# Attention and gated layers on one core: the weight comparison moved ahead of the first exponentials, the second key fill moved to ScalarE, the last norm split over two steps

## The chip, the cores and the metric

The kernel runs on one core of a Trainium2 chip. A core has five engines that run their own instruction streams and wait for each other through semaphores: TensorE (PE in the profile: matrix products and transposes, results in PSUM), VectorE (DVE), ScalarE (ACT: activation functions), GpSimd (POOL) and SyncE (SP, which here only starts DMA transfers). ACT starts DMAs too. The metric is the device time of one execution in microseconds; lower is better.

## The reference

32 sequences of 256 tokens, 128 features. One causal attention layer of 16 heads of 8 features with a linear decay, a residual and a layer norm; then a chain of five scaled linear layers, a residual and a second norm. All in float32.

```python
Q, K, V = (split_heads(x @ W.T + b) for W, b in ((Wq, bq), (Wk, bk), (Wv, bv)))
scores = einsum('bhid,bhjd->bhij', Q, K) / sqrt(8)
scores = where(j > i, -inf, scores) - (i - j)        # decay by distance
out = (softmax(scores) @ V).reshape(B, T, D) @ Wo.T + bo
x = layernorm(x + out)
h = silu((x @ w1.T) * s1) * ((x @ w2.T) * s2)        # 128 -> 512
h = gelu((h @ h1.T) * sh1)                           # 512 -> 512
h = gelu((h @ h2.T) * sh2)                           # 512 -> 512
x = layernorm(x + (h @ w3.T) * s3)                   # 512 -> 128
```

The matrices `w1`, `w2`, `h1`, `h2`, `w3` come out of the setup with whole-number entries.

## The kernel before

**Tiles.** Two sequences make a *pair* (512 tokens); there are 16 pairs, and the main loop is `step(n)` for n = 0 to 15. For each pair the queries and keys of all heads lie in two large tiles, `qs` and `ks` (128 partitions x 8 groups x 512 tokens), of which there are two each, used in turn by even and odd pairs. A head takes 8 rows of features, each stored as a rounded part and a remainder (`qhi`, `qlo`, `khi`, `klo`), further rows with constants that bring in the decay, and two rows for the row maxima. The constant rows are written once into each of the four tiles by `fill`; `stack` then copies a pair's features into their rows with four DMAs of 256 KB for q and four for k.

**One pair's work.**
- `project(n)`: loads the x of pair n + 1, transposes x (`pxT`, `xT`), multiplies by Wq and Wk (`pq`, `pk`) and splits the results into `hi` (ACT) and `lo` (DVE). POOL adds the bias `bo` to x.
- `row_maxima(n, i)`, i = 0 to 11: scores in one orientation into a PSUM tile, then a DVE reduction to `m` (the profile's `m<-s`). `maxima_to_rows(n)`: transposes `m` (`pm`), splits it (`mhi`, `mlo`) and copies it with DMAs into the rows of `qs`.
- `weigh(n, i)`, i = 0 to 11: scores in the other orientation with the maxima taken off, exp on ACT (`e`), causal zeroing on POOL (`e<-e`). Score tiles and the tiles of the layers share three PSUM buffers of two banks, in turn.
- `outputs(n, a)`: `e` times the values (`pa`), a copy (`oT`), a transpose (`pt`), the division (`rec`, `on`). `project_values` makes the values (`pv`, `vaug`).
- `finish(n)`: transposes `on` (`pon`, `onT`), multiplies by Wo (`po`) and adds x. `first_norm(n)`: statistics (`sta`, `mva`, `rsa`), a power on POOL, the scaled x. `turn(n)`: its transpose (`px1T`, `x1T`).
- `feed(n)`: the four 512-wide layers on `x1T`: `pw` and `sg`, `h0w`, `h`; then `podd`, `hodd` and `peven`, `heven`. With exact weights the activations are again a rounded part and a remainder, made by ACT (twice) and DVE (the remainder), and every product has both.
- `last(n)`: the `w3` product (`pw` on `heven`), a copy `yT`, a transpose `py`, the residual `y`, the last norm (`stf`, `mvf`, `rsf`, a power on POOL, `z`) and the store of `z`.

**Order.** There is no planner at work: engines keep the order in which the program issues instructions, which is written out by hand with generators. `step(n)` first runs twelve slots: in slot i it weighs tile i of pair n, takes maximum tile i of pair n + 1, and lets `project(n + 2)`, `last(n - 2)` and the outputs advance at given slots. Then it runs `feed(n - 1)`; between two pieces of it one piece of `rest()` is issued, in this order: the remaining outputs, `maxima_to_rows(n + 1)`, the values of pair n + 2, `finish(n)`, `first_norm(n)` and what is left of `last(n - 2)`, that is its norm's statistics in one slot and `z` in the next. `LEAD` and `LAG` shift the maxima: 2 tiles of pair 1 come before step 0, and in step 1 the maxima of pair 2 start 3 slots late, the last three go into `rest`.

**The opening.** Before the loop come the constants, `project(0)`, the fills, the stacks of pairs 0 and 1, and the maxima of pair 0. `ks0` is filled by ACT, `qs0` and `qs1` by DVE, `ks1` by POOL. The weight matrices are loaded (`load_layers`, SP) in the middle of the maxima of pair 0.

**The branch on the weights.** `inexact_weights` rounds the five matrices, in 11 pieces of 512 columns (ACT copies `w_near`, `h_near`), compares each with its original (DVE, `differ`) and counts the differences into `number`. Its pieces are issued between the slots of step 0. After step 0, which has no `feed`, each engine loads `number` and branches: with no difference the rounded weights are used as they are (this is the branch taken with these inputs), otherwise full float32 weights are loaded again. Steps 1 to 15 are inside the branch.

**DMA.** SP and ACT each issue in order. Eight completion semaphores are used in turn by both, so that a DMA is issued only when the one eight places before it has landed.

Of the kernel before, what the change touches and what calls it, by code (L numbers as in the profile page):

```python
# [33 lines left out]
G, C = 4, 4  # L34


LEAD, LAG = 2, 3
VHEAD = HD + 1
VSLOT = 3 * VHEAD
VCOLS = H // 2 * VSLOT + 32 + VHEAD - VSLOT  # L40
HID = 512
# [20 lines left out]
def tile_attn_ffn(  # L62
# [47 lines left out]

    qs = [const.tile([P, W, TOK], F32R, name=f"qs{i}") for i in range(2)]
    ks = [const.tile([P, W, TOK], F32R, name=f"ks{i}") for i in range(2)]
    sctx = ctx.enter_context(ExitStack())
    setup = sctx.enter_context(tc.tile_pool(name="setup", bufs=1))

# [111 lines left out]
    for i in range(2):  # L227
# [7 lines left out]


    layers = (
        ("w1", w1T, 1, HID), ("w2", w2T, 1, HID), ("h1", h1T, KC, HID), ("h2", h2T, KC, HID),
        ("w3", w3T, KC, D),
    )  # L240
    near = {
        nm: const.tile([P, k, o], F32R, name=f"{nm}_near") for nm, _, k, o in layers
# [3 lines left out]
        sc[nm] = const.tile([P, KC], F32, name=nm)  # L246
    sc["s3"] = const.tile([P, 1], F32, name="s3")

    def load_layers(pool):
        got = {}  # L250
        for nm, src, k, o in layers:
            got[nm] = pool.tile([P, k, o], F32, name=f"{nm}_sb")
            sp.dma_start(out=got[nm], in_=src.rearrange("(k p) o -> p k o", p=P))
        return got
# [412 lines left out]
    def run(gen):  # L667
        for _ in gen:
            pass


    ahead = project(0)
    next(ahead)
    constants("q", q)
    fill(qs[0], "q", vec)
    run(ahead)
    stack(0, "q", sp)
    stack(0, "k", act)
    fill(ks[1], "k", nc.gpsimd)
    ahead = project(1)  # L680
    next(ahead)
    fill(qs[1], "q", vec)
    run(ahead)
    stack(1, "q", sp)
    stack(1, "k", act)
    project_values(0)
    for a in range(G):
        act.dma_start(
            out=wo_sb[C * HD * a : C * HD * (a + 1), :],
            in_=woT[:, :, a, :].rearrange("c d o -> (c d) o"),  # L690
        )
    sctx.close()
    ep = enter(tc.tile_pool(name="ep", bufs=5))
    op = enter(tc.tile_pool(name="op", bufs=2))
    yp = enter(tc.tile_pool(name="yp", bufs=2))
    lctx = ctx.enter_context(ExitStack())
    once = lctx.enter_context(tc.tile_pool(name="once", bufs=1))
    for i in range(6):
        row_maxima(0, i)
    project_values(1)  # L700
    maxima_to_rows(0, (0,))
    loaded = load_layers(once)
    for i in range(6, 3 * G):
        row_maxima(0, i)
    maxima_to_rows(0, (1,))
    load_scales()
    for i in range(LEAD):
        row_maxima(1, i)

    def step(n, exact=None, ws=None, hp=None, gp=None):  # L710


        side = iter(())
        settling = (
            last(n - 2, exact, ws, gp) if n > 1 else first_norm(0) if n else inexact_weights()
        )
        ahead = project(n + 2) if n + 2 < NPAIR else iter(())
        for i in range(3 * G):
            weigh(n, i)
            j = i + {0: LEAD, 1: -LAG}.get(n, 0)  # L720
            if n + 1 < NPAIR and 0 <= j < 3 * G:
                row_maxima(n + 1, j)
            next(side, None)
            if n and i == 9:
                turn(n - 1, exact)
            if i in ((0, 2) if n > 1 else (0, 2, 4, 6)) if n else i < 11:
                next(settling, None)

            if i in ((3, 4, 5) if n == 1 else (1, 3, 5)):
                next(ahead, None)  # L730
            if i % 3 == 2:
                run(side)
                side = outputs(n, i // 3)
            if n == 0 and i == 3 * G - LEAD:
                maxima_to_rows(1)
        if n < 2:
            run(settling)
        run(ahead)
        if n + 2 < NPAIR:
            stack(n + 2, "q")  # L740
            stack(n + 2, "k", sp if n else act)


        def rest():
            for _ in range(3):
                next(side)
                yield
            if n == 1:
                for i in range(3 * G - LAG, 3 * G):
                    row_maxima(2, i)  # L750
                    yield
            if 0 < n < NPAIR - 1:
                maxima_to_rows(n + 1)
            run(side)
            yield
            if n + 2 < NPAIR:
                project_values(n + 2)
                yield
            last_steps = finish(n)
            next(last_steps)  # L760
            yield
            yield from last_steps
            if n:
                yield
                yield from first_norm(n)
            if n == NPAIR - 1:
                yield
                turn(n, exact)
            if n > 1:
                yield  # L770
                yield from settling

        if n:
            prepare(AF.Silu)
        due = rest()
        for _ in feed(n - 1, exact, ws, hp, gp) if n else ():
            next(due, None)
        run(due)

    def others(exact, ws, hp, gp):  # L780
        for n in range(1, NPAIR):
            step(n, exact, ws, hp, gp)

        settling = last(NPAIR - 2, exact, ws, gp)
        for i, _ in enumerate(feed(NPAIR - 1, exact, ws, hp, gp)):
            if i in (3, 4, 8, 9):
                next(settling, None)
        run(last(NPAIR - 1, exact, ws, gp))

    step(0)  # L790
    inexact = nc.values_load(
        pairs.pop("inexact"), min_val=0, max_val=P * HID * 11,
        skip_runtime_bounds_check_because="it is only compared with zero",
# [68 lines left out]
```

## Time and profile before

| | |
|---|---|
| time, median of 3 runs | 848.8 us (848.36 to 851.17) |
| the profiled execution's own time | 849.53 us |
| its span, first to last instruction | 847.2 us |
| mean granted TensorE clock | 0.978 |
| busy: PE, DVE, ACT, POOL | 789.4, 642.9, 525.1, 276.1 us |
| DMA moved | 47.49 MB |
| ACT table loads | 47 of 1283 ns |
| maxima reductions, 128 | 155.5 us, 1218 ns each |
| exponentials, 128 | 130.5 us, 1020 ns each |
| one step in the middle, start to start | 48.74 us |
| first maxima product; first product of steps 0, 1, 2 | 30.02; 49.74, 85.79, 136.80 us |

A line of the timeline gives the start in us from the span's start, the duration, the engine, the source line (L58 is a helper that issues most instructions), the operation, output <- inputs by the program's names, the shapes, a count, and in brackets the engine's idle time before it with what ended it. PEld is the loading of weights into TensorE. A window line gives the stretch and its length, then the busy time of PE, PEld, DVE, ACT and POOL with their instruction counts, the granted TensorE clock, the busy share of the DMA engines and GB/s. In the table of slices each digit is one fortieth of the span, in tenths.

### The profile page before, as it was taken

To read this page: it belongs to the slowest core of one execution; us is meant where nothing else is said; L and a number is where in the kernel's file an instruction comes from. 1 tells how busy PE (TensorE), PEld (TensorE's weight loads), DVE (VectorE), ACT (ScalarE), POOL (GpSimd) and SP (SyncE) were. 2 spreads that over 40 slices of the span, in tenths; PEclk is the share of its full clock that TensorE was granted. 3 is DMA by queue.
4 is the path that set the end of the run, shared out by engine and by line. 5 is a ranking of instruction groups with operands and counts; after the bars stand their busy time and mean duration, and the time that the engine had idled before them with its cause. 6 is when DMAs were issued, how large, how long until landed. Compare 5 with 4: busy or idle time off the path is not lost.

```text
span 847.2 us, 17426 instructions
## 1 busy us (share of the span) xinstructions
PE 789.4 (93%) x7046; PEld 553.1 (65%) x7046; DVE 642.9 (76%) x1245; ACT 525.1 (62%) x718; POOL 276.1 (33%) x341
## 2 busy tenths in 40 slices
PE   2897899999999999999999999999999999999985
PEld 0555576676767677676767667676766767666663
DVE  8877777877787777778878777878878777773674
ACT  3036565766666666666667676667667666668662
POOL 9023422414142432414243341424234141424210
PEclk9859999999999999999999999999999999999998
DMA  2843140411314040220404031040414013000001
GB/s 65 197 146 80 38 102 15 93 36 29 76 26 103 27 101 28 49 56 26 103 26 104 26 73 44 15 103 27 104 26 94 23 26 79 14 4 13 1 13 30
DMA packets 39882, 47.49 MB, mean 56 GB/s; under 512 B 3952, under 2 KB 21616, under 8 KB 39792
## 3 DMA queue, kind: packets, MB, share of 16 engines
q1 hardware_dynamic: 37136, 42.82, 21.3%
q10 hardware_dynamic: 2656, 3.48, 1.7%
q8 instruction: 57, 0.93, 0.5%
q14 instruction: 33, 0.27, 0.1%
HBM read 7.48 MB, written 4.19 MB: 14 GB/s over the span
## 4 chain that ended last, share of the span: by engine, by line
PE 73%; DVE 10%; ACT 4%; POOL 3%; issue 1%; DMA 1%; SPq 0%; ACTq 0%; POOLq 0%; DVEq 0%
PE podd L58 13%; PE pa L58 11%; PE s L58 10%; PE peven L58 8%; PE pw L58 8%; DVE heven L58 4%; POOL rsf L273 2%; PE s_2d L58 2%; PE s_3d L58 2%; PE s_1d L58 2%; PE s_0d L58 2%; PE po L58 2%; DVE z L58 2%; PE pt L58 2%; PE pk L58 2%; PE pq L58 2%
## 5 line engine op out<-in xcount | busy, mean ns | idle before, releaser
L58 DVE TENSOR_REDUCE m<-s 128x4 f32<-128x1024 f32 x128 | 155.5, 1218 | 9.1 <-PE s L58 7.8
L58 ACT ACTIVATE e<-s 128x1024 f32<-128x1024 f32 x128 | 130.5, 1020 | 45.0 <-PE s L58 25.4
L462 POOL TENSOR_SCALAR_AFFINE_SELECT e<-e 128x512 f32<-128x512 f32 x128 | 84.7, 662 | 184.3 <-ACT e L58 156.2
L58 PE MATMUL podd<-h,h_near 128*128 128x512 f32 x512 | 131.4, 403 | 0.9 <-DVE m L58 0.5
L58 PE MATMUL peven<-hodd,h_near 128*128 128x512 f32 x512 | 122.6, 395 | 0.0
L58 PEld LDWEIGHTS peven<-hodd,h_near 128*128 128x128 f32 x512 | 95.8, 187 | 23.2
L58 PEld LDWEIGHTS podd<-h,h_near 128*128 128x128 f32 x512 | 91.8, 188 | 23.0 <-DVE h L58 3.0
L58 ACT ACTIVATE hodd<-podd,sh 128x512 fp32r<-128x512 f32 x64 | 44.0, 688 | 62.8 <-PE podd L58 62.6
L58 PE MATMUL pw<-x1T,w_near 128*128 128x512 f32 x256 | 75.6, 418 | 2.2 <-DVE h0w L58 2.2
L273 POOL TENSOR_TENSOR rsa<-rsa,half 128x4 f32<-128x4 f32 x16 | 16.3, 1018 | 175.9 <-DVE rsa L58 175.9
L58 PE MATMUL pa<-e,vaug 128*32 128x256 f32 x1024 | 71.4, 393 | 0.0
L58 DVE SCALAR_TENSOR_TENSOR h0w<-pw,s,sg 128x512 f32<-128x512 f32 x64 | 47.9, 748 | 29.4 <-ACT sg L58 29.4
L58 PEld LDWEIGHTS s<-qs,ks 64*128 64x128 f32 x512 | 38.9, 188 | 47.3 <-issue 33.6
L58 DVE TENSOR_TENSOR heven<-evenw,heven 128x512 fp32r<-128x512 f32 x64 | 44.0, 688 | 29.5 <-ACT evenw L58 29.0
L58 PE MATMUL s<-qs,ks 64*128 64x256 f32 x512 | 65.3, 334 | 1.1 <-DMA qs<-qhi 0.6
L58 ACT ACT_TABLE_LOAD x47 | 60.3, 1283 | 3.4 <-issue 2.6
L58 ACT ACTIVATE sg<-pw,s 128x512 f32<-128x512 f32 x64 | 43.6, 683 | 29.0 <-PE pw L58 27.9
L58 PE MATMUL s<-ks,qs 62*128 62x256 f32 x512 | 55.1, 294 | 4.0 <-ACT e_0d L58 1.7
L58 ACT ACTIVATE heven<-peven,sh 128x512 fp32r<-128x512 f32 x48 | 33.3, 694 | 39.7 <-PE peven L58 39.7
L58 PEld LDWEIGHTS pw<-x1T,w_near 128*128 128x128 f32 x256 | 43.4, 188 | 19.5 <-ACT nothing L58 5.8
L580 POOL TENSOR_TENSOR h<-h0w,h 128x512 fp32r<-128x512 f32 x31 | 39.9, 1288 | 43.5 <-DVE h L58 41.2
L273 POOL TENSOR_TENSOR rsf<-rsf,half 128x4 f32<-128x4 f32 x16 | 21.0, 1314 | 97.1 <-DVE rsf L58 97.1
(148 smaller groups left out, 1462.4 us busy)
## 6 DMA issues: line engine op xcount, KB each, us to landing
qs<-qhi SPq DMA_DIRECT2D x32, 256.0 KB
qs<-qlo SPq DMA_DIRECT2D x32, 256.0 KB
ks<-khi SPq DMA_DIRECT2D x26, 256.0 KB
ks<-klo SPq DMA_DIRECT2D x26, 256.0 KB
x<-in_x_dram SPq DMA_DIRECT2D x16, 256.0 KB
out_dram<-z SPq DMA_DIRECT2D x16, 256.0 KB
ks<-khi ACTq DMA_DIRECT2D x6, 256.0 KB
ks<-klo ACTq DMA_DIRECT2D x6, 256.0 KB
```

The source lines that it names most:

```text
L58: return lambda *args, **kw: self.tc.keep_in_program_order(call(*args, **kw))
L273: nc.gpsimd.tensor_tensor(rs, rs, half, ALU.pow)
L462: nc.gpsimd.affine_select(out=on_diagonal, in_=on_diagonal, pattern=[[0, on_diagonal.shape[1]], [1, P]], base=0, channel_multiplier=-1, co ...
L580: (nc.gpsimd if o < (1 if final else 2) else vec).tensor_tensor(h[:, 1, o, :], whole, h[:, 0, o, :].bitcast(F32), ALU.subtract)
```

## The change

- **Fills.** `ks1` is filled by ACT instead of POOL, after three pieces of the comparison. 
- **Weights.** `w1`, `w2`, `w3` are loaded by SP right behind the x of pair 1, `h1` and `h2` behind the first q stack. `wo` and the scales go to SP behind the second q stack. The order of the layers in the comparison becomes w1, w2, w3, h1, h2.
- **Comparison and branch.** All 11 pieces are issued in the opening: three before the first maxima, six after maxima tiles 6 to 11 of pair 0, two after the first two maxima tiles of pair 1. The count, the load of `number` and the branch follow, and step 0 is now inside the branch.
- **Step 0 to step 1.** Step 0 ends after its twelve slots; its last outputs, the values of pair 2, `finish(0)` and `first_norm(0)` are issued one piece a slot in step 1 (`attended`). `stack(2, "k")` moves from ACT to SP. `LAG` is 5 instead of 3, the five maxima tiles left go into three pieces of `rest`, and `project(3)` moves from slots 3, 4, 5 of step 1 to slots 6, 7, 8.
- **Last norm.** In `rest` the statistics of `last(n - 2)` and the power are issued in the same slot as the end of `first_norm(n)`; `z` and its store wait in `late` until slot 3 of the next step (after the loop for the last one).

```diff
-LEAD, LAG = 2, 3
+LEAD, LAG = 2, 5
...
     ahead = project(0)
     next(ahead)
+    loaded = load_layers(once, layers[:3])
     constants("q", q)
     fill(qs[0], "q", vec)
     run(ahead)
     stack(0, "q", sp)
     stack(0, "k", act)
-    fill(ks[1], "k", nc.gpsimd)
+    loaded.update(load_layers(once, layers[3:]))
+    comparison = inexact_weights()
     ahead = project(1)
     next(ahead)
     fill(qs[1], "q", vec)
+    for _ in range(3):
+        next(comparison)
+    fill(ks[1], "k", act)
+    for i in range(2):
+        row_maxima(0, i)
+    next(ahead)
+    row_maxima(0, 2)
     run(ahead)
     stack(1, "q", sp)
     stack(1, "k", act)
+    row_maxima(0, 3)
     project_values(0)
+    for i in range(4, 6):
+        row_maxima(0, i)
...
+    load_scales()
+    project_values(1)
     sctx.close()
...
     maxima_to_rows(0, (0,))
-    loaded = load_layers(once)
     for i in range(6, 3 * G):
         row_maxima(0, i)
+        next(comparison)
+    prepare(AF.Exp)
     maxima_to_rows(0, (1,))
-    load_scales()
     for i in range(LEAD):
         row_maxima(1, i)
+        next(comparison)
+    run(comparison)
+    late, left = [], []
+    def attended(n, side):
+        yield from side
+        project_values(n + 2)
+        yield
+        last_steps = finish(n)
+        next(last_steps)
+        yield
+        yield from last_steps
+        yield from first_norm(n)
...
+            if i == 3 and late:
+                run(late.pop())
...
-            if i in ((3, 4, 5) if n == 1 else (1, 3, 5)):
+            if i in ((6, 7, 8) if n == 1 else (1, 3, 5)):
                 next(ahead, None)
...
-            stack(n + 2, "k", sp if n else act)
+            stack(n + 2, "k")
+        if n == 0:
+            left.append(side)
+            return
...
-            if n:
-                yield
-                yield from first_norm(n)
+            yield
+            yield from first_norm(n)
...
             if n > 1:
-                yield
-                yield from settling
+                next(settling)
+                late.append(settling)
...
     def others(exact, ws, hp, gp):
-        for n in range(1, NPAIR):
+        for n in range(NPAIR):
             step(n, exact, ws, hp, gp)
+        run(late.pop())
...
-    step(0)
     inexact = nc.values_load(
```

More of the change, by code (lines that the diff above doesn't have):

```diff
@@ L112, in tile_attn_ffn @@
     ks = [const.tile([P, W, TOK], F32R, name=f"ks{i}") for i in range(2)]
+    ep = enter(tc.tile_pool(name="ep", bufs=5))
+    op = enter(tc.tile_pool(name="op", bufs=2))
+    yp = enter(tc.tile_pool(name="yp", bufs=2))
+    lctx = ctx.enter_context(ExitStack())
+    once = lctx.enter_context(tc.tile_pool(name="once", bufs=1))
     sctx = ctx.enter_context(ExitStack())
@@ L237, in tile_attn_ffn @@
     layers = (
-        ("w1", w1T, 1, HID), ("w2", w2T, 1, HID), ("h1", h1T, KC, HID), ("h2", h2T, KC, HID),
-        ("w3", w3T, KC, D),
+        ("w1", w1T, 1, HID), ("w2", w2T, 1, HID), ("w3", w3T, KC, D), ("h1", h1T, KC, HID),
+        ("h2", h2T, KC, HID),
     )
@@ L247, in tile_attn_ffn, with load_layers @@
     sc["s3"] = const.tile([P, 1], F32, name="s3")
-    def load_layers(pool):
+    def load_layers(pool, some=layers):
         got = {}
-        for nm, src, k, o in layers:
+        for nm, src, k, o in some:
             got[nm] = pool.tile([P, k, o], F32, name=f"{nm}_sb")
@@ L685, in tile_attn_ffn @@
     stack(1, "k", act)
+    row_maxima(0, 3)
     project_values(0)
+    for i in range(4, 6):
+        row_maxima(0, i)
     for a in range(G):
-        act.dma_start(
+        sp.dma_start(
             out=wo_sb[C * HD * a : C * HD * (a + 1), :],
@@ L691, in tile_attn_ffn, with step @@
         )
+    load_scales()
+    project_values(1)
     sctx.close()
[L693 to L700, printed above, removed]
     maxima_to_rows(0, (0,))
-    loaded = load_layers(once)
     for i in range(6, 3 * G):
         row_maxima(0, i)
+        next(comparison)
+    prepare(AF.Exp)
     maxima_to_rows(0, (1,))
-    load_scales()
     for i in range(LEAD):
         row_maxima(1, i)
-    def step(n, exact=None, ws=None, hp=None, gp=None):
+        next(comparison)
[10 more added lines that the diff above has]
+        yield from first_norm(n)
+    def step(n, exact, ws, hp, gp):
         side = iter(())
         settling = (
-            last(n - 2, exact, ws, gp) if n > 1 else first_norm(0) if n else inexact_weights()
+            last(n - 2, exact, ws, gp) if n > 1 else attended(0, left.pop()) if n else iter(())
         )
@@ L725, in step @@
                 turn(n - 1, exact)
-            if i in ((0, 2) if n > 1 else (0, 2, 4, 6)) if n else i < 11:
+            if n < 2 or i in (0, 2):
                 next(settling, None)
-            if i in ((3, 4, 5) if n == 1 else (1, 3, 5)):
+            if i in ((6, 7, 8) if n == 1 else (1, 3, 5)):
                 next(ahead, None)
@@ L750, in rest @@
                     row_maxima(2, i)
-                    yield
-            if 0 < n < NPAIR - 1:
+                    if i % 2:
+                        yield
+            if n < NPAIR - 1:
                 maxima_to_rows(n + 1)
@@ L762, in rest @@
             yield from last_steps
-            if n:
-                yield
-                yield from first_norm(n)
+            yield
+            yield from first_norm(n)
             if n == NPAIR - 1:
@@ L769, in rest @@
             if n > 1:
-                yield
-                yield from settling
-        if n:
-            prepare(AF.Silu)
+                next(settling)
+                late.append(settling)
+        prepare(AF.Silu)
         due = rest()
-        for _ in feed(n - 1, exact, ws, hp, gp) if n else ():
+        for _ in feed(n - 1, exact, ws, hp, gp):
             next(due, None)
```

## The prediction

> **What bounds the kernel now.** I read the table of 40 slices, then windows, the timeline at one handover between steps, and the opening.
>
> ```profile
> PE   2897899999999999999999999999999999999985
> PEclk9859999999999999999999999999999999999998
> ```
> From slice 5 on TensorE (PE) is full: there it is the bound, and only its own stalls can be won. A window over one step:
> ```profile
> 427.88:476.62 48.74, 47.90 (x442) 33.81 (x442) 38.16 (x76) 32.31 (x44) 16.25 (x21) 1.00 0.24 56
> ```
> 48.74 us a step; VectorE (DVE) holds 38.16, ScalarE (ACT) 32.31. The timeline shows where PE stops:
> ```profile
> 427.60 1.38 POOL L273 TENSOR_TENSOR rsf<-rsf,half 128x4 f32<-128x4 f32 x1 [5.27 <-DVE rsf L58]
> 427.88 0.51 PE L58 MATMUL s<-qs,ks 64*128 64x256 f32 x4
> 429.01 1.12 DVE L58 TENSOR_SCALAR z<-y,mvf,rsf 128x128 f32<-128x128 f32 x4 [0.91 <-POOL rsf L273]
> 430.05 0.68 DVE L58 TENSOR_TENSOR heven<-evenw,heven 128x512 fp32r<-128x512 f32 x1
> 430.79 0.84 PE L58 MATMUL pw<-heven,w_near 128*128 128x512 f32 x2 [0.61 <-DVE heven L58]
> 431.85 0.49 PE L58 MATMUL pw<-heven,w_near 128*128 128x512 f32 x1 [0.22 <-DVE heven L58]
> 432.27 0.50 PE L58 MATMUL s<-qs,ks 64*128 64x256 f32 x4
> ```
> DVE waits for POOL's power and writes the last norm's z while two `heven` remainders queue behind it; PE's `w3` product (pw) waits for those. The step from pair 1 to 2 has no such norm in front:
> ```profile
> 136.80 0.50 PE L58 MATMUL s<-qs,ks 64*128 64x256 f32 x4
> 137.65 2.13 PE L58 MATMUL pw<-heven,w_near 128*128 128x512 f32 x8
> 139.71 0.50 PE L58 MATMUL s<-qs,ks 64*128 64x256 f32 x4
> ```
> 2.91 us from the first s to the second, against 4.39.
>
> The opening is bound by a DVE held up beside POOL, and the stacks' transfers:
> ```profile
> 5.58 10.62 POOL L192 TENSOR_SCALAR ks<-kconst,col_k_base 128x4096 fp32r<-128x4096 f32 x1
> 5.83 10.65 DVE L58 TENSOR_SCALAR qconst<-number_of,col_q_lo,col_q_value 128x512 f32<-128x512 f32 x1
> 30.02 0.50 PE L58 MATMUL s<-ks,qs 62*128 62x256 f32 x4 [1.32 <-DMA qs<-qlo]
> 77.59 0.14 DVE L58 CAST number<-total 1x1 int32<-1x1 f32 x1
> 85.79 0.74 PE L58 MATMUL s<-qs,ks 64*128 64x256 f32 x8 [0.58 <-DMA qs<-qhi]
> ```
> The same DVE operation on kconst took 0.58 at 2.13. Step 0 runs 49.74 to 85.79.
>
> **The change, part by part.** Times are in the profiled execution, 849.53 us (span 847.2 and 2.3 around it), 0.7 above the median, 848.8.
>
> *Second k fill to ACT.* Without POOL's 10.62, qconst's three operations (0.6 + 0.8 + 0.8) start at 5.83 and the q fill (2.43) ends near 10.5, not 20.66. The eight stack transfers (2.1 MB) are then issued 10.6 to 13.2; at 0.24 MB/us (the 22 to 30 us rows give 220 to 253 GB/s) they land at 20.9, and with as much delay as the first ones showed, 21.5. First maxima matmul 21.5 instead of 30.02: -8.5. ACT's fill (3.71 as its sister at 5.67) and three weight copies (0.61 each) end by 19, under the transfers; uncovered they cost 5.5.
>
> *Weights.* w1, w2, w3 (0.79 MB) go out on SP behind x; h1, h2 (2.1 MB) and x of pair 2 behind the first q stack. Within the queue they follow it: 0. Bound: served ahead of it, 2.36 MB at 286 GB/s (the 44 to 46 row, weights moving) costs 8.2. `wo` and the scales move from ACT to SP, behind the second q stack; the maxima rows queue behind them, but are read only at 52, and `wo` in step 1: 0, or the 5.14 that ACT's four `wo` issues took.
>
> *Comparison and branch ahead of step 0.* Between the first maxima and the branch DVE now has 14 maxima (two in 2.34: 16.4), 8 comparisons (69.28 to 71.03 is one with a maximum, 1.79 typical, so 0.62: 5.0), qlo and klo 1.5, v additions 2 x 0.89, mlo 2 x 0.68, the count 0.3: 26.4. Waits (0.7 for the first tile, qlo and klo behind products of 1.0 to 2.05, two mlo behind 1.0 to 1.6) are 1.8 to 5; I take 3.6, as PE is mostly slow here. The number stands at 51.5. Load and branch now stand in front of all: `x` ending at 86.01 and its statistics starting at 86.08 bound them below at 0.1, po's first matmul (84.05) to s (85.79) above at 1.7; I take 1.2, nearer PE's row. Step 0 starts at 52.7, +3.0 on 49.74.
>
> *Step 0 without comparisons.* PE's work to the end of pm, by the durations of the chain: 11 score tiles (8 at 0.43, 3 diagonal ones at 0.61) 5.3, 10 maxima tiles (6 at 0.42, 4 at 0.66) 5.2, the projection (0.59, 1.06, 1.06) 2.7, pa three times 1.00 + 0.57, 4.7, pt 0.6, pm 0.4: 18.9 at full clock. DVE has 15.2 of work beside it (10 maxima, xT, qlo, klo, one rec and on) and ACT 14.8 (11 exps, qhi, khi, oT, mhi), so both fit under PE; before it took 25.8 (49.74 to 75.52), half of that at clock 0.50:
> ```profile
> 32.00:34.00 2.00, 2.00 (x20) 1.21 (x20) 2.00 (x2) 0.00 (x0) 0.00 (x0) 0.50 1.07 228
> 58.00:62.00 4.00, 4.00 (x20) 1.23 (x22) 1.87 (x5) 0.56 (x2) 0.62 (x1) 0.50 0.00 0
> ```
> The clock was 0.50 for 6.4 us (from 31.9), 20.4 (from 42) and 3 (from 89.9). PE is sparse before the branch, so step 0 starts slow; I take 8.4 us, half of it lost: 4.2 (bounds 1.5 and 10.2). pm ends at 75.8.
> The Trainium skill (TensorE: Matmul & The Clock Gate, What's actually happening) says that one sustained busy window of about 3.4 us restores the full clock. The stretch at 89.9 agrees, the two longer ones, full by their rows, do not; by the rule the sum would be 2.5 lower, 827.5.
>
> *Hand-over 0 to 1.* Nothing of pair 0 stands before step 1's first s now, so it meets mhi, mlo and their transfers: 1.9 to mlo's issue (75.52 to 77.64 without the comparison between), and a landing of 0.6 to 3.3 (x: issue 0.79, read 4.10); I take 2: s at 79.7, not 85.79, though PE stands idle for some 3 us before it. The k stack on SP frees ACT of the 3.04 it waited at 77 to 80.
>
> *Step 1.* It takes over pa's end (1.57), pt, pv, pon, po from step 0 and the branch: 4.6 of PE work. Up to `pw` PE holds 12 score tiles 5.9, seven maxima tiles 3.4, pa 6.3, two pt 1.2, pv, pon, po 2.4, the projection 2.7, px1T 0.6: 22.5; the maxima of pair 2, five tiles later, still meet their stacks: issued from pm + 3.3, 9.0 to move, 2 to land is 90.1 (the 80 to 86 rows move 0.23 MB/us); PE, 8.2 into the step, is there at 87.9: 2.2 of waiting, and 0.6 of small waits like the 0.2 to 0.8 ones of step 1 now. pw at 105.0 (108.82 before). Its feed layers took 28.0; two more maxima tiles there (1.1) and podd's wait for their buffers (1.0) make 30.1: step 2 starts at 135.1 instead of 136.80. All before step 2: **-1.7**.
>
> *Last norm.* Its statistics now follow the first norm's x in DVE's gap (423.55 to 425.56), z goes behind the fourth maximum of the next step, where the line of qlo at 439.30 shows DVE idle for 1.22: z's 1.12 fits, price 0, at most 1.12. SP issues its store after the next x. heven runs as in the pair 1 to 2 step, whose second diagonal tile comes 4.47 after the first s (136.80, 141.27) against 5.83 (427.88, 433.71): 1.36 less. Next late is exp behind ACT's table load. Pairs 2 to 13 hand over so: 12 x 1.36 = **-16.3**. The hand-over 14 to 15 ends on ACT: 0. In the last step z (1.11 at 811.34) leaves its place before three heven operations but comes again before h0w; with sg, freed 0.4 earlier, h0w starts near 813.2 instead of 814.03: **-0.8**.
>
> Sum -18.8: 849.53 - 18.8 - 0.7 = **830.0**.
>
> **Rivals.**
> 1. *Weights in front of the stacks.* The transfer rows of 22 to 38 us are full, so sharing is real; queue order speaks against it. +8.2: 838.2.
> 2. *The clock comes back in 3 us*, as at 89.9, here and in the comparisons (products 1.06, not 2.05): -2.7 and -2.7: 824.6. Against it: two of the three slow stretches lasted longer. The rule of the Trainium skill (TensorE: Matmul & The Clock Gate, What's actually happening) would have it so.
> 3. *The stall only moves*: z's 1.12 pushes maxima whose buffers PE waits for, and the 16.3 come back: 846.3. Against it: the 1.22 gap.
> 4. *Slower: the clock stays halved* through step 0 and on. It decides from 46 us of slow dense work (8.4 + 2 x 18.8); the longest stretch seen is 20.4. Lasting to step 1's pw (41.4 of work, all lost again, less the 4.2) it gives 867.
> 5. *No change in effect*: none; the instruction order does move z, fill and branch.
>
> **Numbers.** Forecast 0.50, rivals 0.20, 0.20, 0.05, 0.05. A measurement tells about 0.3%; 846.3 is within it. Faster 0.90, same 0.05, slower 0.05. Range 820 (rival 2, with the short waits and early landing) to 841 (rival 1, with late branch and landing).
>
> **What would show it.** s after the first hand-over s: 2.9 us, step period 47.4; z without idle POOL wait near qlo; qconst at 0.6; first maxima near 21.5; the number near 51.5; step 1's s near 80; step 2 near 135. Wrong if PE waits appear on DVE m after z, or the granted clock is 0.50 beyond 70 us.

## The result, and the profile after

The changed kernel takes 839.25 us (median of 4 runs, 838.77 to 841.65); the kernel before took 849.98 beside it (4 runs, 848.36 to 854.79). The ratio is 0.987, with a 95% interval of 0.9824 to 0.9916: faster by 1.3%. 830.0 was forecast, with a range of 820 to 841. The profiled execution took 838.77 us, with a span of 836.9, so 10.3 us of span came off where 18.8 were forecast.

The trace gives the two halves of that apart. In the steady part everything came as forecast. The page's table of 40 slices for the changed kernel:

```profile
PE   2868899999999999999999999999999999999995
...
PEclk9959899999999999999999999999999999999998
```

One window over a step of it, from first s to first s:

```profile
428.08:475.49 47.41, 47.41 (x442) 33.89 (x442) 38.35 (x76) 32.23 (x44) 15.69 (x20) 1.00 0.25 58
```

And the timeline of the same hand-over that was shown of before:

```profile
425.08 1.01 POOL L278 TENSOR_TENSOR rsf<-rsf,half 128x4 f32<-128x4 f32 x1 [2.58 <-DVE rsf L58]
...
428.08 0.51 PE L58 MATMUL s<-qs,ks 64*128 64x256 f32 x4
...
428.93 2.11 PE L58 MATMUL pw<-heven,w_near 128*128 128x512 f32 x8
...
430.98 0.50 PE L58 MATMUL s<-qs,ks 64*128 64x256 f32 x4
...
436.85 1.11 DVE L58 TENSOR_SCALAR z<-y,mvf,rsf 128x128 f32<-128x128 f32 x4
438.16 0.75 DVE L58 SCALAR_TENSOR_TENSOR qlo<-pq,bq_sb,qhi 128x512 fp32r<-128x512 f32 x1 [0.20 <-ACT qhi L58]
```

The step is 47.41 us long, TensorE (PE) is busy in all of it (in the table of slices, from slice 6 on but for the last), the eight `pw` products follow each other without a stop, and the second s comes 2.90 us after the first (4.39 before). The power runs beside `heven`, and `z` lies in VectorE's gap ahead of `qlo`, which now shows 0.20 of idle time.

The opening, in single lines of the timeline on VectorE and TensorE:

```profile
5.79 0.54 DVE L58 TENSOR_SCALAR qconst<-number_of,col_q_lo,col_q_value 128x512 f32<-128x512 f32 x1
21.98 0.80 PE L58 MATMUL s<-ks,qs 62*128 62x256 f32 x4 [9.86 <-DMA ks<-klo]
53.43 0.14 DVE L58 CAST number<-total 1x1 int32<-1x1 f32 x1
54.47 0.80 PE L58 MATMUL s<-qs,ks 64*128 64x256 f32 x4 [1.26 <-DVE number L58]
81.49 0.50 PE L58 MATMUL s<-qs,ks 64*128 64x256 f32 x4 [2.67 <-DMA qs<-mlo]
93.64 0.50 PE L58 MATMUL s<-ks,qs 62*128 62x256 f32 x4 [0.66 <-issue]
```

They read: `qconst` freed from POOL; first maxima; the count of differing weights; first s of step 0 behind the branch; first s of step 1 behind `mlo`'s transfer; first maxima of pair 2. The first s of step 2 stands at 143.73, 6.9 us later than before (136.80), where 1.7 earlier was forecast. So the steady part gave 17.2 (from there to the end 693.2 us instead of 710.4; 17.1 forecast) and the opening took 6.9 of it back. What follows is about those 6.9.

Two things in step 1 were not in the forecast. Windows of 3.41 us show the granted clock (the column before the last two) fall to 0.50 three times:

```profile
79.06:82.47 3.41, 0.98 (x16) 0.70 (x20) 0.49 (x1) 1.27 (x2) 1.09 (x1) 1.00 0.05 19
82.47:85.88 3.41, 3.41 (x40) 1.96 (x32) 0.00 (x0) 2.20 (x3) 1.21 (x2) 0.50 0.94 226
85.88:89.30 3.42, 3.42 (x28) 1.91 (x26) 0.85 (x3) 2.05 (x2) 1.32 (x3) 0.50 1.07 229
...
99.53:102.95 3.42, 1.75 (x14) 0.99 (x14) 2.75 (x5) 1.17 (x2) 1.53 (x4) 1.00 0.27 73
102.95:106.36 3.41, 3.41 (x16) 1.55 (x14) 1.88 (x2) 1.10 (x2) 1.09 (x1) 0.50 0.01 4
...
123.43:126.84 3.41, 2.33 (x36) 1.66 (x34) 2.75 (x3) 2.24 (x4) 0.00 (x0) 1.00 0.03 5
126.84:130.25 3.41, 3.41 (x15) 2.49 (x14) 3.06 (x4) 0.00 (x0) 0.00 (x0) 0.50 0.01 2
```

And VectorE makes TensorE wait in slot 6, because the scaled `x` of pair 0's first norm is issued ahead of the copy `xT`:

```profile
98.84 1.71 DVE L58 TENSOR_SCALAR x<-x,mva,rsa 128x128 f32<-128x128 f32 x4
100.47 0.68 DVE L58 COPY xT<-pxT 128x512 f32<-128x512 f32 x1
...
101.20 1.12 PE L58 MATMUL pq<-xT,wq_sb 128*128 128x512 f32 x2 [1.71 <-DVE xT L58]
```

So there were two theories of the missing time. *Clock*: half clock behind each bare stretch makes step 1 long. *Order and transfers*: TensorE waits for pair 2's stacks, and later for `xT`, and the clock falls in time that is lost anyway. A third possibility was that the two halves of the change disturb each other.

### The profile page after: what moved, and what is told of

It is laid out like the page before. It is cut to its first block, busy times and chain, and to the rows that moved or that the text cites. A ratio compares the mean times of both kernels' runs of the same rounds, so it can differ in the third digit from the quotient of the medians.

```text
span 836.9 us, 17426 instructions
## 1 busy us (share of the span) xinstructions
PE 786.9 (94%) x7046; PEld 555.4 (66%) x7046; DVE 634.8 (76%) x1245; ACT 528.7 (63%) x720; POOL 257.7 (31%) x340
## 4 chain that ended last, share of the span: by engine, by line
PE 84%; DVE 6%; ACT 3%; issue 1%; POOL 0%; DMA 0%; ACTq 0%; POOLq 0%; DVEq 0%
PE peven L58 14%; PE podd L58 13%; PE s L58 12%; PE pa L58 12%; PE pw L58 10%; PE s_0d L58 2%; PE s_3d L58 2%; PE s_1d L58 2%; PE s_2d L58 2%; PE pt L58 2%; PE po L58 2%; PE pk L58 2%; PE pq L58 2%; PE pv L58 2%; DVE m L58 1%
## 5 line engine op out<-in xcount | busy, mean ns | idle before, releaser
L467 POOL TENSOR_SCALAR_AFFINE_SELECT e<-e 128x512 f32<-128x512 f32 x128 | 81.6, 637 | 238.9 <-ACT e L58 238.9
L58 PE MATMUL s<-ks,qs 62*128 62x256 f32 x512 | 57.0, 302 | 12.7 <-DMA ks<-klo 9.9
L278 POOL TENSOR_TENSOR rsa<-rsa,half 128x4 f32<-128x4 f32 x16 | 16.3, 1018 | 170.2 <-DVE rsa L58 170.1
L58 PEld LDWEIGHTS s<-ks,qs 62*128 62x128 f32 x512 | 41.2, 195 | 17.9 <-issue 12.0
```

The costliest lines, as they stand in the source:

```text
L58: return lambda *args, **kw: self.tc.keep_in_program_order(call(*args, **kw))
L278: nc.gpsimd.tensor_tensor(rs, rs, half, ALU.pow)
L467: nc.gpsimd.affine_select(out=on_diagonal, in_=on_diagonal, pattern=[[0, on_diagonal.shape[1]], [1, P]], base=0, channel_multiplier=-1, co ...
```

## The experiments

The starts of the first s in the profiled execution of each kernel, in us, and the time from step 2's start to the end of the span. Times are medians, each with its ratio to the kernel before in the same series of runs. The labels are those of the sections below. The medians of the kernel before lay between 848.8 and 850.0 us in all series, so where two changed kernels are compared, the difference of their medians is given.

| kernel | step 0 | step 1 | step 2 | rest | time | ratio (95%) |
|---|---|---|---|---|---|---|
| before | 49.74 | 85.79 | 136.80 | 710.4 | | |
| after | 54.47 | 81.49 | 143.73 | 693.2 | 839.25 | 0.9870 (0.9824 to 0.9916) |
| e1 norm alone | 51.00 | 87.07 | 140.12 | 693.3 | 831.91 | 0.9788 (0.9772 to 0.9805) |
| e2 opening alone | 54.63 | 81.52 | 143.99 | 711.5 | 857.14 | 1.0088 (1.0071 to 1.0104) |
| e3 fill alone | 42.74 | 77.88 | 130.19 | 711.5 | 842.86 | 0.9913 (0.9895 to 0.9930) |
| e4 dense filler | 56.34 | 83.82 | 146.24 | 693.4 | 840.85 | 0.9895 (0.9878 to 0.9911) |
| e5 norm and fill | 42.78 | 78.37 | 129.70 | 693.2 | 824.62 | 0.9713 (0.9697 to 0.9730) |
| e6 old hand-over | 54.76 | 88.42 | 141.88 | 693.3 | 837.47 | 0.9868 (0.9852 to 0.9885) |
| e7 xT first | 55.00 | 82.15 | 141.20 | 693.3 | 836.53 | 0.9857 (0.9841 to 0.9874) |
| e8 LAG 8 | 54.97 | 82.23 | 145.81 | 693.2 | 842.49 | 0.9924 (0.9908 to 0.9941) |
| e9 dense opening | 54.92 | 81.64 | 143.99 | 693.2 | 842.06 | 0.9933 (0.9908 to 0.9958) |
| e10 short comparison | 51.18 | 78.22 | 140.79 | 693.1 | 835.81 | 0.9848 (0.9831 to 0.9864) |
| e11 norm, fill, dense | 43.62 | 78.83 | 128.88 | 693.2 | 825.69 | 0.9731 (0.9715 to 0.9747) |
| e12 k stack on ACT | 54.56 | 83.27 | 147.68 | 693.1 | 843.63 | 0.9934 (0.9913 to 0.9954) |

The column "rest" holds two groups: 693.1 to 693.4 with the last norm moved, 710.4 to 711.5 without. Whatever the opening does, nothing of it is given back or lost behind step 2. The kernels can therefore be read by where step 2 starts.

### The two halves apart: e1 and e2

e1 takes the kernel before and moves the last norm only:

```diff
+            if i == 3 and late:
+                run(late.pop())
...
             if n > 1:
-                yield
-                yield from settling
+                next(settling)
+                late.append(settling)
...
             step(n, exact, ws, hp, gp)
+        run(late.pop())
```

> The kernel before with the last norm's move alone (statistics in the slot of the first norm's end, z and its store in slot 3 of the next step); fills, weights, comparison, branch and step 0 as before. Theory: the steady gain is whole and independent of the opening, so step 2 still starts at 136.8, the step period is 47.4 instead of 48.74, and the profiled time is 849.5 - 17.1 = 832.4, some 6 to 7 us less than the full change. Rival: z's new place needs the new opening (buffers in other turns, the maxima shifted by LAG), so that part of the 17 does not appear: 834 to 839.

Measured: 831.91 us against 849.58, 17.7 less, and the step is as long as in the changed kernel. The theory holds and the rival falls. One thing is odd: the profiled execution, at 835.72 the slowest of four (the others took 830.91, 830.91 and 832.92), reached step 2 at 140.12, 3.3 us later than the kernel before, although both issue the same instructions up to there. It had the granted clock at 0.50 from 91.4 to 98.4, the kernel before from 89.7 to 93.1. An opening of one and the same kernel thus varies by some 3 us, and the starts in the table carry that much of chance.

e2 is the changed kernel with that part undone:

> The changed kernel with the last norm put back where it was (all of the opening's edits stay). Theory: the opening as rewritten costs 6.9 us up to step 2 and nothing gives it back: step 2 starts at 143.7, period 48.74, profiled time 849.5 + 6.9 = 856.4, slower than before. Rival: the 6.9 is absorbed in the steps behind (a later start of step 2 meets buffers and loads that are then ready): 849 to 852.

Measured: 857.14 us, 7.6 more than before (849.58). The rewritten opening alone makes the kernel slower, as the theory said. And -17.7 + 7.6 = -10.1 is close to the whole change's -10.7 (839.25 against 849.98): the halves add, they do not disturb each other.

### The fill: e3 and e5

```diff
-    fill(ks[1], "k", nc.gpsimd)
+    fill(ks[1], "k", act)
```

> The kernel before with one edit: ks1 is filled by ACT instead of POOL, in the same place. Theory: VectorE's operation on kconst for q takes 0.6 instead of 10.65 us, the first maxima product is at 21.5 to 22 instead of 30.02, and what follows is bound by VectorE's work and shifts as a whole: step 0 starts at 41 to 43, step 2 at 128 to 130, time 841 to 843. Rival: the shift is taken back by the transfers (weights and the second pair's stacks then meet the first stacks on the same rings) or by the granted clock, and step 2 starts within 3 us of 136.8: time 846 to 850.

Measured: 842.86 us, 6.7 less than before; first maxima at 22.01, step 0 at 42.74, step 2 at 130.19. The theory holds: of 8.0 us at the first maxima 7.0 arrive at step 0 and 6.6 at step 2, and nothing of it goes to the transfers. So the fill is worth -6.7 of the opening's +7.6, and all else in the opening (loads, comparison, branch, hand-over) costs 14.3.

e5 puts the two gains together, on the kernel before:

> The kernel before with two parts of the change: the last norm's move and ks1 filled by ACT; comparison, branch, loads, step 0 and its hand-over stay as they were. Theory: the two gains lie at different places and add: 849.6 - 17.7 - 6.7 = 825.2, faster than both kernels. Rival: part of the fill's 6.7 only shows while step 2 is late for another reason, and the sum stops at 828 to 832.

Measured: 824.62 us (824.08 to 825.53), where 825.2 was worked out. This is the fastest of all, 2.9% faster than the kernel before and 1.6% faster than the whole change (0.9713 / 0.9870 = 0.984).

### The hand-over, and what stands ahead of step 0: e6 and e10

e6 is the changed kernel with pair 0's last outputs, the values of pair 2 and `finish(0)` back at the end of step 0:

```diff
-LEAD, LAG = 2, 5
+LEAD, LAG = 2, 3
...
-            last(n - 2, exact, ws, gp) if n > 1 else attended(0, left.pop()) if n else iter(())
+            last(n - 2, exact, ws, gp) if n > 1 else first_norm(0) if n else iter(())
...
-            if n < 2 or i in (0, 2):
+            if i in ((0, 2) if n > 1 else (0, 2, 4, 6)):
...
-            if i in ((6, 7, 8) if n == 1 else (1, 3, 5)):
+            if i in ((3, 4, 5) if n == 1 else (1, 3, 5)):
...
         if n == 0:
-            left.append(side)
+            run(side)
+            project_values(n + 2)
+            run(finish(n))
             return
...
                     row_maxima(2, i)
-                    if i % 2:
-                        yield
+                    yield
```

> The changed kernel with the hand-over from step 0 to step 1 as before: pair 0's last outputs, the values of pair 2 and the Wo product run at the end of step 0, LAG 3, the projection of pair 3 in slots 3 to 5; comparison and branch stay ahead of step 0, the k stack of pair 2 stays on SP. Theory: the new hand-over saves nothing, since the maxima of pair 2 wait for stacks that can only start when step 0's scores are done, and idle time that the old tail filled with work is now bare: step 0 starts at 54 to 56, steps 0 and 1 take 84 to 87 us together instead of 89.3, time 834 to 838. Rival: the new hand-over is worth what was forecast (4.7 less than the old 87.06) and what was lost is lost elsewhere: steps 0 and 1 take 90 to 95 us, time 840 to 845.

Measured: 837.47 us; steps 0 and 1 together take 141.88 - 54.76 = 87.1 us, against 89.3 in the changed kernel. The new hand-over, with the LAG that goes with it, costs about 2; steps 0 and 1 were to become 4.7 shorter. More is to be seen beside e5. e5 has eleven pieces of comparison and the branch inside steps 0 and 1, e6 has neither there, and by the starts in the table the two steps take 86.9 us in e5 and 87.1 in e6. So the comparison and the branch cost nothing that shows in the sum of the two steps where they stood, beside the half-clocked products of step 0 and the serial tail behind it. A cost of a few us is not excluded: the two kernels also differ in the queue of pair 2's k stack and in where the clock falls, and an opening varies by some 3 us.

In front of step 0, e6 needs 12.0 us more, and the times differ by 12.9. The comparison is only a part of that. VectorE's timeline shows another, the remainders of pair 1's projection. In e5 they lie ahead of the first maxima (22.05), while the stacks are being moved:

```profile
19.17 0.75 DVE L58 SCALAR_TENSOR_TENSOR qlo<-pq,bq_sb,qhi 128x512 fp32r<-128x512 f32 x1 [3.92 <-ACT qhi L58]
19.84 0.74 DVE L58 SCALAR_TENSOR_TENSOR klo<-pk,bk_sb,khi 128x512 fp32r<-128x512 f32 x1
```

In e6 they lie behind the first maxima (22.10), and VectorE waits for them:

```profile
26.89 0.75 DVE L58 SCALAR_TENSOR_TENSOR qlo<-pq,bq_sb,qhi 128x512 fp32r<-128x512 f32 x1 [1.34 <-ACT qhi L58]
...
30.30 0.75 DVE L58 SCALAR_TENSOR_TENSOR klo<-pk,bk_sb,khi 128x512 fp32r<-128x512 f32 x1 [1.49 <-ACT khi L58]
...
54.76 0.80 PE L58 MATMUL s<-qs,ks 64*128 64x256 f32 x4 [1.26 <-DVE number L58]
```

By an estimate from such rows, some 5 of the 12.0 us are then the eight pieces of comparison that are left behind the first maxima, 4.3 the two remainders with their waits, and 2.6 the branch: e5's first s comes 1.7 us before VectorE is through with the first two maxima tiles of pair 1 (44.48), e6's 0.9 us behind `number` (53.87). Only the comparison's part was tested by itself.

e10 does that, with only 32 of 512 columns compared:

```diff
-                differ = once.tile([P, HID], F32, name=f"differ_{at}", tag="differ")
+                differ = once.tile([P, 32], F32, name=f"differ_{at}", tag="differ")
                 vec.scalar_tensor_tensor(
-                    differ, whole, 1.0, part.bitcast(F32), ALU.mult, ALU.not_equal,
+                    differ, whole[:, 0:32], 1.0, part[:, 0:32].bitcast(F32), ALU.mult, ALU.not_equal,
```

> The changed kernel with 32 of 512 columns compared in each of the eleven pieces (the other columns are not compared, so this kernel leaves out most of the test of the weights; the roundings by ACT stay). Theory: ahead of step 0 VectorE is the bound and the comparison is bare there: eight pieces of 0.67 become some 0.13, number comes 4 to 5 us earlier, and the time falls by 4 to 5 to 834 to 835.5. Rival (roundings on ACT, the maxima's products at half clock or the weights' landing set the pace): number less than 2 us earlier, 837 to 839.5.

Measured: 835.81 us, 3.4 less than the changed kernel; `number` at 50.14 instead of 53.43, step 2 at 140.79. Eight pieces went from 0.67 to 0.17, 4.0 in sum, and 3.3 of it reached `number`. That is less than the 4 to 5 us expected, and more than the rival allows: VectorE is the bound there, and the comparison stands bare.

### Clock or transfers in step 1: e4, e9 and e12

e4 fills the bare stretch between steps 0 and 1 with products:

```diff
         if n == 0:
+            warm = two("warm")
+            for _ in range(2):
+                pe.matmul(
+                    warm[:, 0, :], lhsT=wq_sb, rhs=pairs[2]["xT"], start=True, stop=True
+                )
             left.append(side)
             return
```

> The changed kernel with two more products on TensorE (Wq times the x of pair 2, 1.06 us each at full clock, results not used) between the last score tile of step 0 and the first of step 1, where TensorE stood idle 2.67 us for mlo's transfer. Clock theory: the granted clock fell to 0.50 at 82.5 for 6.75 us because the 3.4 us before held only 0.98 us of products; with the filler it stays 1.00 there, step 1's first score product is within 0.4 of 81.5, its pw comes about 3 us earlier than 112.3, step 2 starts near 140.7 and the time is 835.8. Rival (waits and added work make step 1 long, the clock does not matter): step 2 at 143.7 to 144.2, time 838.8 to 839.3.

Measured: 840.85 us, no gain. The granted clock stayed at 1.00 where it falls in the changed kernel, but it fell behind the next wait, from 95.6 to 102.4, so that from step 1's first s to step 2 it was at 0.50 for 10.2 us, against 13.6. TensorE's timeline, from the filler to the first maxima of pair 2:

```profile
81.08 1.98 PE L58 MATMUL warm<-xT,wq_sb 128*128 128x512 f32 x4
83.82 0.50 PE L58 MATMUL s<-qs,ks 64*128 64x256 f32 x4 [0.76 <-DMA qs<-mlo]
...
92.22 0.66 PE L58 MATMUL s_1d<-qs,ks 64*128 64x128 f32 x8
95.69 0.80 PE L58 MATMUL s<-ks,qs 62*128 62x256 f32 x4 [2.81 <-DMA ks<-klo]
```

TensorE is ready for the maxima 2.4 us sooner after the step's start than in the changed kernel (92.22 + 0.66 - 83.82 = 9.1, against 11.5 with its two windows at half clock), and then waits 2.81 for `klo`. The way from step 1's first s to the first maxima of pair 2 is 11.9 us here and 12.15 in the changed kernel. In e2 and e9 the clock was at 0.50 there for one window and not two, and the way was 12.3 and 12.2, with waits of 2.31 and 2.19 for `klo`. What sets this stretch is the landing of the stacks, which SP issues behind the maxima rows (from 81.53 on in the changed kernel), once step 0's last scores (78.16) have read the tiles; the clock's first fall hides in that wait. What a full clock through all of step 1 would give, e4 does not show. Its four executions speak against much: with mean granted clocks of 0.959, 0.959, 0.961 and 0.990 they took 841.28, 841.41, 840.06 and 840.41 us.

e9 fills the waits in the opening in the same way (`warm` is one PSUM tile of the pool `work`, `more` multiplies Wq with the x of pair 1 into it):

```diff
+    warm(0, 1)
     maxima_to_rows(0, (0,))
+    more = warm(1, 0)
     for i in range(6, 3 * G):
         row_maxima(0, i)
+        more(1)
         next(comparison)
+    more(2)
     prepare(AF.Exp)
     maxima_to_rows(0, (1,))
+    more = warm(2, 0)
     for i in range(LEAD):
         row_maxima(1, i)
+        more(1)
         next(comparison)
+    more(1)
```

> The changed kernel with eleven-odd products more on TensorE in the opening (Wq times the x of pair 1, results not used): one before pm, one after each maxima tile from 6 on, two and one more where TensorE waited 3.76 and 2.99 us for VectorE. Clock theory: the granted clock, 0.50 from 38.1 to 65.3 in the changed kernel, stays 1.00 there; number stays within 0.7 of 53.5 as VectorE sets it; step 0 to the end of pm takes 19 to 21 us instead of 23.75, the rest shifts, time 834.5 to 837. Rival (VectorE, ACT and the exponentials set step 0's pace, the clock hardly matters): step 0 to pm takes 22.5 to 24, time 838 to 841.

Measured: 842.06 us, slower than the changed kernel rather than faster. The clock stood at 1.00 up to 55.1, but fell there, behind the wait for `number` and the branch, and came back at 65.5, as in the changed kernel (65.4). Windows of e9 around the branch:

```profile
48.00:52.00 4.00, 4.00 (x26) 1.97 (x25) 2.84 (x5) 1.61 (x3) 0.00 (x0) 1.00 0.02 8
52.00:55.00 3.00, 0.98 (x6) 0.22 (x4) 1.61 (x5) 0.00 (x0) 0.00 (x0) 1.00 0.00 0
55.00:60.00 5.00, 5.00 (x42) 3.99 (x42) 3.05 (x3) 2.05 (x2) 2.11 (x5) 0.52 0.20 56
60.00:65.00 5.00, 5.00 (x43) 3.05 (x42) 2.45 (x2) 2.05 (x2) 2.54 (x4) 0.50 0.00 2
```

The changed kernel's three windows in step 0:

```profile
55.17:58.58 3.41, 3.41 (x30) 2.56 (x27) 1.98 (x2) 2.05 (x2) 0.95 (x2) 0.50 0.26 77
58.58:61.99 3.41, 3.41 (x30) 2.85 (x28) 2.29 (x3) 1.60 (x2) 2.96 (x6) 0.50 0.02 5
61.99:65.41 3.42, 3.42 (x24) 1.23 (x22) 1.23 (x1) 0.45 (x1) 0.74 (x2) 0.50 0.01 2
```

So step 0 ran at half clock as long as without the products: the stop at `number` and the branch (0.98 us of products in the window from 52) is enough to bring the fall, even behind a dense stretch. Whether a full clock would shorten step 0, e9 can't say, since it did not give one. Why its median lies 2.8 above the changed kernel's, while its profiled execution (839.02, the lowest of four that reach 844.68) is as long, stays open. The profiled execution also has the highest mean clock of the four (0.983; the others 0.961 to 0.969), so what it shows of the clock need not hold for the others.

e12 undoes one small part, the queue of pair 2's k stack:

```diff
-            stack(n + 2, "k")
+            stack(n + 2, "k", sp if n else act)
```

> The changed kernel with one thing undone: pair 2's k stack is issued by ACT again, beside SP's q stack, and not behind it. Theory (SP's queue makes the stacks late): SP's eight issues run from 81.5 to 87.7, 0.62 us each; with ACT issuing four of them the last lands some 2 us sooner, the first maxima product of pair 2 is at 91 to 92 (93.64 in the changed kernel), step 2 starts 1 to 2.5 us earlier, time 836.5 to 838. Rival (the transfer itself sets it, 2.1 MB at some 0.24 MB/us, 8.7 us): first maxima product within 0.7 of 93.6, time 838.5 to 839.5, or later where ACT's exponentials queue behind the four issues: 840 to 841.5.

Measured: 843.63 us, 4.4 slower than the changed kernel and slower than either theory said. The queues' and TensorE's timelines:

```profile
79.15 1.35 ACTq L58 DMA_DIRECT2D ks<-khi  x2
79.73 0.51 SPq L58 DMA_DIRECT2D qs<-mlo  x1
80.36 0.50 SPq L58 DMA_DIRECT2D qs<-mhi  x1
80.61 2.43 ACTq L58 DMA_DIRECT2D ks<-klo  x2
80.91 1.08 SPq L58 DMA_DIRECT2D qs<-mlo  x1
83.27 0.80 PE L58 MATMUL s<-qs,ks 64*128 64x256 f32 x4 [4.32 <-DMA qs<-mlo]
```

With its own queue the k stack goes out ahead of the small `mhi` and `mlo` rows (16 KB each, the stacks' pieces 256 KB), and TensorE waits 4.32 us for `mlo`, not 2.67; ACT waits 4.09 behind its issues before its next exponential. No wait for the stacks is left (the first maxima of pair 2 follow at 95.83 without one), but nothing is gained by it: the way from step 1's first s to them is 12.6 us, with the granted clock at 0.50 until 92.9 (89.3 in the changed kernel), and a second fall lasts 6.8 us instead of 3.4. Step 2 starts 3.95 us later than in the changed kernel; 1.8 of it is there at step 1's first s, and 2.2 comes behind it, where the clock is at 0.50 for some 20 us and not 13.6. Here, with the stacks there early, TensorE itself is the one awaited, and the half clock may cost; no run parts that from the wait for `xT`, which is 2.16. The move of this stack to SP pays 4.4 us, which the forecast did not have as a term of its own.

### The order on VectorE, and LAG: e7 and e8

e7 issues the projection's pieces of slots 6 to 8 in step 1 ahead of `attended`'s:

```diff
+            if n == 1 and i in (6, 7, 8):
+                next(ahead, None)
             if n < 2 or i in (0, 2):
                 next(settling, None)
 
-            if i in ((6, 7, 8) if n == 1 else (1, 3, 5)):
+            if n != 1 and i in (1, 3, 5):
                 next(ahead, None)
```

The projection also starts the load of pair 4's x, into the buffer where pair 0's residual still waits for its norm. So this kernel computes pair 0's norm from the wrong x; the operations, their sizes and their order on the engines are what the time is read for.

> The changed kernel with one order changed in slots 6 to 8 of step 1: the projection of pair 3 (its copy xT on VectorE) is issued ahead of first_norm(0)'s scaled x, not behind it. Theory (VectorE's order): the 1.71 us in which TensorE waited for xT at 99.5 to 101.2 goes, and with it the drop of the granted clock at 102.95 for 3.4 us, worth 1.5: step 1's pw comes 2 to 3.2 us earlier, step 2 likewise, time 835.5 to 837. Rival (VectorE is full there, so that another tile is late instead): within 0.5 of 838.8.

Measured: 836.53 us, 2.7 less. The lines on VectorE and TensorE:

```profile
99.16 0.68 DVE L58 COPY xT<-pxT 128x512 f32<-128x512 f32 x1
...
99.89 1.12 PE L58 MATMUL pq<-xT,wq_sb 128*128 128x512 f32 x2
100.35 1.72 DVE L58 TENSOR_SCALAR x<-x,mva,rsa 128x128 f32<-128x128 f32 x4 [0.52 <-DMA x<-in_x_dram]
```

TensorE's wait is gone, and the granted clock is 1.00 from 90.3 to the end of step 1's feed part: the falls at 102.95 and 126.84 are gone with it. Steps 0 and 1 take 86.2 us instead of 89.3. Here, where no transfer hides it, a wait of 1.71 brought a half-clocked window behind it, and taking it away gave more than the wait, although 1.26 came back as a wait of `pk` for `qlo`. Of the 2.7, how much is wait and how much is clock the run does not part.

e8 lets the maxima of pair 2 start later still:

```diff
-LEAD, LAG = 2, 5
+LEAD, LAG = 2, 8
```

> The changed kernel with LAG 8 instead of 5: the maxima of pair 2 start three slots later in step 1, eight of them go into the feed part. Theory (stacks): TensorE no longer reaches the maxima before the stacks have landed at 93.6, its pw moves forward by the three maxima tiles (2.0 us) and by the wait of 0.7 to 2.8, but the feed part gets them back: step 2 starts 0 to 2 us earlier, time 837 to 839. Rival (the maxima of pair 2 are VectorE's 1.22 each and make the feed part VectorE-bound, podd's buffers late): step 2 starts 1 to 4 us later, 840 to 843.

Measured: 842.49 us, 3.2 slower: the rival's number, and its mechanism in part. The maxima of pair 2 no longer meet their stacks, but the wait for `xT` became 3.57 us, with the clock at 0.50 from 100.5 to 107.3 behind it, and in the feed part TensorE waits 0.99 for `h0w` and 0.72 for a maximum, both on VectorE. Of the 1.3 us by which step 1 with its feed part is longer in the profiled execution (the lowest of four, 840.82), 0.8 lies ahead of `pw` and 0.5 behind it.

### Filler on the best version: e11

e11 is e5 with the same kind of products in its opening:

```diff
+    warm(0, 1)
     maxima_to_rows(0, (0,))
     loaded = load_layers(once)
+    more = warm(1, 0)
     for i in range(6, 3 * G):
         row_maxima(0, i)
+        more(1, T)
```

> The kernel before with the last norm's move, ks1 filled by ACT, and products on TensorE whose results are not used: one of 512 columns before pm of pair 0, one of 256 columns after each of the maxima tiles 6 to 11. Clock theory: the stretch at clock 0.50 from 35.4 to 56 shrinks to 10 us or less, step 0 to pm (42.8 to 68.2 without the products) takes 21 to 23 us instead of 25.4, time 820 to 823 against 824.6. Rival (step 0 with the comparison in it is VectorE's, 1.22 + 0.75 us a slot): 824 to 827.

Measured: 825.69 us, within its interval no different from e5. The stretch at clock 0.50 shrank from 20.4 us (35.5 to 55.9) to 7.0 (46.3 to 53.3), and step 0 to the start of `pm` from 25.4 us to 23.7, between the two theories. But step 0 starts 0.8 later, a second fall lasts 6.8 us (70.3 to 77.1) instead of 3.4, and step 2 starts only 0.8 earlier in the profiled execution. 10 us less of half clock up to there were worth next to nothing. That fits the rival, for which VectorE paces step 0 when the comparison is in it.

## Why the prediction was right, and where its sum was not

The forecast was faster, 830.0; it became 839.25, near the upper end of 820 to 841. That end was rival 1's 8.2 us for the weights, with a late branch and a late landing. Rival 1 did not occur, and the sum missed by 8.5 us of span for other reasons, all of them ahead of step 2; that the time still lies inside the range is luck. The direction rests on the last norm alone: the opening, put at a gain of 1.7, lost 6.9. One of the prediction's own signs of being wrong came: the granted clock was 0.50 beyond 70 us, from 82.47 to 89.30.

- *Last norm, -16.3 and last step, -0.8.* Right to 0.1: the period is 47.41 (47.4), the rest from step 2 on is 17.2 shorter, and e1 shows 17.7 of time for this part alone. z did find its gap, so rival 3 falls.
- *Second k fill.* Right: first maxima at 21.98 (21.5), `qconst` 0.54. e3 adds that it is worth 6.7 alone.
- *Weights.* Right at a price of nothing: the first maxima were not late, so rival 1 falls.
- *Comparison and branch ahead of step 0.* The step start was 54.47 instead of 52.7. The first s was 0.5 late, VectorE's work from there to the count came to 25.6 (26.4), the load and the branch to 0.9 (1.2, from the end of `number`'s cast to s); the term that was too small is the waits, 5.9 instead of 3.6: 1.10 for the first tile, 1.33 and 1.49 for `qhi` and `khi` behind products (`pq`, `pk`) that took 2.07 us and not 1.12, 0.51 and 1.11 for two `mhi`, and 0.39 for the count.
- *Step 0.* 54.47 to pm's end at 78.22 is 23.75, against 23.1. The half clock lasted 10.9 us of it (8.4), so rival 2, a clock back in 3 us, falls.
- *Hand-over.* 3.3 us from pm's end to s, against 3.9. Right; e12 shows that this hangs on the k stack standing behind `mlo` in one queue.
- *Step 1, 25.3 to its `pw`.* This is the step that failed: 30.8 (81.49 to 112.27). Its first half missed by 1.75: the maxima of pair 2 began 12.15 after the step's start instead of 10.4, and e2, e4 and e9 show that the stacks' landing, not the clock, sets that (the forecast had the wait for the stacks, too small). Its second half missed by 3.7 (18.6 from those maxima to `pw`, against 14.9): the small waits put at 0.6 were 1.71 for `xT` and 0.78 for `klo`, and a window at half clock followed. e7 shows that the order of `x` and `xT` on VectorE stands behind it, worth 2.7 of time with what hangs on it in the feed part (31.5 instead of 30.1; 30.2 in e7).
- *All before step 2, -1.7.* It came out at +6.9. The sum credited the new steps 0 and 1 with 82.4 us against 87.06 before; e6 with the old hand-over takes 87.1, and e5 with comparison and branch inside takes 86.9. What the comparison's leaving takes off step 0 (26.0 us to pm's end in e5, 23.8 in e6) is back in step 1 (51.3 and 53.5, with one and two windows at half clock in it; that the clock makes this difference is not shown), and the forecast had counted the first without the second. Rival 4, a clock that stays halved, was wrong as it was put, but its effect was there in pieces: 13.6 us of half clock in step 1 and its feed part, of which the first 6.8 hid in the wait for the stacks.

## What to carry to other kernels

Before a piece of work is moved to the front of a serial stage, ask what it costs where it stands: the comparison and the branch cost nothing that shows beside step 0, and with them ahead of it and pair 1's projection behind the first maxima, the stretch up to step 0 grew by 12 us. When work is pushed into the next stage, follow its order on the second engine and not only on the bound one: one scaled x ahead of one copy cost 2.7 us. And a change made of parts is best measured by parts: here one part gave 17.7 us, one 6.7, and the rest cost 14.3, so that the two good parts alone beat the whole by 14.6 us.

## What the runs showed of the hardware

The granted clock changes on a grid. In the changed kernel its record changes at 38.1, 65.4, 82.5, 89.3, 103.0, 106.4, 126.8 and 130.3 us, and all differences are multiples of 3.41 within 0.1; in the kernel before the stretches at 0.50 lasted 6.7, 20.5 and 3.4. The Trainium skill (TensorE: Matmul & The Clock Gate, What's actually happening) says that the window is 3413 ns long and free-running, so that the place in it varies from run to run; the grid agrees, and the 3.3 us by which the same opening came later in e1's profiled execution fit that, though no run shows it to be the cause. The record is not the whole of it: from 21.98 to about 31 it says 1.00, and products take as long as at 0.50 (the first maxima product 0.80 us, the one at 93.64 0.50).

How many busy windows bring the clock back is another matter. The same section says that it comes back after at least one busy window. Here one window was enough at 102.95 (with `pt` and `pk`) and at 126.84 (with `podd`), two were needed at 82.47, and the last three of the stretch from 38.1, from 55.17 on, were all full, by TensorE's busy time. And a half-idle window does not always take it away; these are windows of the kernel before:

```profile
76.04:79.45 3.41, 1.80 (x36) 0.80 (x34) 1.37 (x5) 1.12 (x2) 1.09 (x1) 1.00 0.46 126
79.45:82.87 3.42, 1.78 (x14) 1.62 (x15) 1.21 (x5) 0.58 (x1) 0.00 (x0) 1.00 0.97 241
82.87:86.28 3.41, 2.05 (x20) 1.65 (x20) 2.02 (x6) 0.00 (x0) 0.00 (x0) 1.00 1.07 221
```

The clock stays at 1.00 through three windows with 1.8 to 2.05 us of products (`pa`, `pt`, `pv`, `pon`, `po`), while 2.33 us of mostly score tiles at 123.43 were followed by half clock. So TensorE's busy time alone does not decide it, and neither does the kind of product: full windows of nothing but score tiles and `pa` restored the clock in e9 (82.49 to 85.90) and did not in the changed kernel (82.47 to 85.88), and one with 2.0 us of `po`, products with 128 rows and 128 columns, did not in e4 (95.62 to 99.03, 3.35 us busy). What decides stays open. What the tests do show is that less half clock gained nothing where TensorE was not the one awaited: e11 took 10 us of it away up to step 2, and its time is no different from e5's.
